# A four-layer kernel on one core: the first half sequence's state-space preparation, issued beside the attention in smaller steps

## The chip, the cores and the metric

One NeuronCore of a Trainium2 chip runs the whole kernel in one launch. The metric is the time of one execution in device microseconds. All arithmetic is fp32. TensorE does the matrix products, VectorE and ScalarE the elementwise work on SBUF and PSUM, GpSimd elementwise work on SBUF and indirect transfers, and SyncE issues most other transfers.

## The reference

Four layers run one after another on x of shape (4, 1024, 128), each an attention-like part and a feed-forward part, with a layer norm behind each part. The change lies where the third layer meets the fourth.

- Layer 2 (the third), first part: a causal linear attention with 16 heads of 64, its queries and keys put through a ReLU and weighted by cos and sin of the position. Second part: a mixture of 8 experts of which each token takes 2.
- Layer 3 (the fourth), first part: a selective state-space model. Each token row is scaled by its root mean square, projected to 256 channels, put through a causal convolution of width 4 and a SiLU; then

```
delta = softplus(wd2 @ (wd1 @ xs) + b)        # 256 channels x time
B, C  = wb @ xs, wc @ xs                       # 16 states x time
h_n(t) = exp(delta(t) * A_n) * h_n(t-1) + delta(t) * xs(t) * B_n(t)
y(t)   = sum_n C_n(t) * h_n(t) + W_D * xs(t)   # gated, projected, added
```

  Second part: 8 experts of width 512 with a top-p choice, computed for every token.

## The kernel before, in words

The sequence of each of the 4 batches is cut in two for layer 3: eight half sequences of 512 tokens. Tokens lie on partitions in `xN[b]`; `xT[b]` is the transposed copy, features on partitions.

**Order of work.** The kernel is a set of Python generators, each of which emits some instructions up to its next `yield`. The loop in `l2_attn` runs over t; one turn is called a unit here. There are 128 units (16 quarters of 256 tokens times 8 pairs of heads), in a pipeline: turn t emits, in this order on TensorE, the transposes of the keys of unit t+1 (`l2_keys`, tile kp_mo), the projection of unit t+2 (`l2_project`, pqk), the scores of t+1 (pa_m, masked by VectorE into `a`), the products with the state and within the block of unit t (po), and the running sums of t+1 (kp_mo, added by VectorE into `st`). Then comes one tile of layer 2's experts for an earlier batch (`early(moe)`), then one call of `begin`, then the division by the normaliser (`l2_out`: dn, co), then the generators in `side`: values of the next quarter (pv), output projection (transposes pt<-co, ScalarE's copy coT, pr), a layer norm, and after a batch's last quarter its dispatch to the experts, which ends in 16 indirect scatters on GpSimd (xrows<-xN). The tile scheduler may reorder what VectorE, ScalarE and GpSimd get, by a plan of the times; in the attention TensorE keeps the written order. Each engine executes its instructions in the order it got them.

`self.beat` is the last ReLU of the newest projection (r_k<-pqk on ScalarE). The scatters already have a dependency on it ("spread out"), so that one goes out with each unit.

**PSUM in the attention.** There are 8 banks: two of tag pj (used by turns for pqk, pv, the transposes pt, the dispatch and the preparation), two for po, one for pr, three for the scores, the keys and sums, and the expert tiles.

**The preparation.** `l3_prepare(u)` makes a half sequence ready for the scan: squares and root mean square (L1754 to L1759), scaling (L1761), transposes and xnT (L1766 to L1769); for each of two groups of 128 channels a projection (pxe), the convolution on VectorE (L1786 to L1802), Tanh (L1806) and xs (L1807); the small projection pdb with db (L1815) and the store of its B and C rows to DRAM (L1816); then for each group delta: the projection pd, softplus as max(p, 0) + log1p(exp(-|p|)) with a correction for rounding (L1826 to L1839), ud = xs * delta (L1840) and the copy of delta to dl (L1841). For seven halves this runs during the scan of the half before. The first half has none before it, so `l2_attn` calls its preparation (`begin`, made by `l3_early`) once a unit as soon as the first batch has left layer 2's experts. `l3_early` places its working tiles in parts of `xT[0]`, `xT[1]`, `xT[2]` that are not read any more. Its PSUM banks are of tag pj, and a bank is worked in until the last step that uses it: the convolution and Tanh stay in pxe, softplus in pd.

**After the attention.** `l3` runs the scans. For every state n GpSimd multiplies ud by a broadcast row of B (L1876: db<-ud,bn; for the first half the tile reads db<-xT,bn), ScalarE takes the exponential (L1880), VectorE scans (L1881), GpSimd multiplies by a row of C (L1892), TensorE sums over n (pys). Layer 2's remaining expert tiles, their gathers on GpSimd (L1556: yg<-yrows) and layer 3's experts (ph, hh, py) are woven in.

Of the kernel before, what the change touches and what calls it, by code (L numbers as in the profile page):

```python
# [42 lines left out]
E3, NST, DDELTA, KCONV = 256, 16, 64, 4  # L43
# [5 lines left out]
SYNC = mybir.DependencyInfo(mybir.DependencyClass.Sync, mybir.DependencyReason.DATA)  # L49
# [22 lines left out]
class Net:  # L72
# [874 lines left out]
    def l2_attn(self, load, dispatch, moe, first):  # L947
# [7 lines left out]
        with ExitStack() as ctx:  # L955
# [35 lines left out]
            for t in range(-2, n + 4):  # L991
                if t == 0:
                    load()
                if 0 <= t + 1 < n:
                    u = units[t + 1]
                    if u["hp"] == 0:
                        i = (t + 1) // NP2
                        if i + 1 < len(quarters):
                            nxt = quarters[i + 1]
                            self.l2_tiles(nxt, quarters[i])  # L1000
                            side.append(self.l2_values(nxt))
                    self.l2_keys(u)
                if 0 <= t + 2 < n:
                    self.l2_project(units[t + 2])
                if 0 <= t + 1 < n:
                    self.l2_scores(units[t + 1])
                if 0 <= t < n:
                    self.l2_before(units[t])
                    self.l2_within(units[t])
                if 0 <= t + 1 < n:  # L1010
                    self.l2_sums(units[t + 1])
                if "put" in self.m2["st"][0] if t > 0 else False:
                    early(moe)
                    if "done" in self.m2["st"][0]:
# [12 lines left out]
                for g in side[:]:  # L1027
                    if next(g, self) is self:
                        side.remove(g)
            for g in (begin, *side):  # L1030
                for f in g:
                    if f == "put":
                        self.m2["rest"] = g
                        break
# [490 lines left out]
    def l2_expert_out(self, u, units, i, wp):  # L1525
# [12 lines left out]
        if j % 4 == n - 1:  # L1538
# [4 lines left out]
                in_=ys[:, 0:n, :],  # L1543
            )

    def l2_combine(self, st, wp):

        nc, b = self.nc, st["b"]
# [172 lines left out]
    def l3_early(self, pool):  # L1721


        half = lambda b, i: self.xT[b][:, i * 512 : (i + 1) * 512]
        k = [0]

        def at(name, shape):
            if name in ("xnT", "tail", "xs3"):
                return pool.tile(shape, F32, name=name)
            if name in ("dl", "ud"):  # L1730
                return self.xT[1 if name == "dl" else 2].rearrange("p (e t) -> p e t", e=2)
            if name == "sq3":
                return half(2, 0).rearrange("p (k d) -> p k d", d=D)
            if name == "db1":
                return half(2, 1)[0:ND]
            if name == "xc":
                k[0] += 1
                return half(0, k[0] % 2)
            return half(0, name == "sp_w")[:, None, :]

        u = dict(b=0, h=0, at=at, ff=self.bank("pj"))
        self.c3["first"] = u
        return u

    def l3_prepare(self, u):
# [2 lines left out]
        at, ff, dp = u.get("at", self.l3_at), u.get("ff", self.bank("ff")), c3["dp"]  # L1748
        wdb = c3["we"][:, :, 0:ND]

        sq = at("sq3", [P, 4, D])
        ms = self.sm.tile([P, 4], F32, name="ms3")
        for k in range(4):
            nc.scalar.activation(  # L1754
                sq[:, k, :], self.xN[b][:, 4 * h + k, :], AF.Square, accum_out=ms[:, k : k + 1]
            )
        yield
        nc.scalar.activation(ms, ms, AF.Sqrt, bias=self.epsc, scale=1.0 / D)
        nc.vector.reciprocal(ms, ms)  # L1759
        for k in range(4):  # L1760
            nc.scalar.activation(  # L1761
                sq[:, k, :], self.xN[b][:, 4 * h + k, :], AF.Copy, scale=ms[:, k : k + 1]
            )
        yield
        pt = ff([P, 4, P], "pt")
        for k in range(4):  # L1766
            self.tr(pt[:, k, :], sq[:, k, :])
# [2 lines left out]
            xnT, pt.rearrange("p a b -> p (a b)"), AF.Copy, scale=self.col("norm_w")  # L1770
        )
        yield

        K1 = KCONV - 1
        tail = at("tail", [P, 2, K1]) if h == 0 else u["prev"]["tail"]
# [2 lines left out]
        for ec in range(2):  # L1778
            p = ff([P, 512], "pxe")
            self.mm(p, c3["wskip"][:, 1, ec * P : (ec + 1) * P], xnT)  # L1780
            xc = at("xc", [P, 512])
            i = 2 * KCONV + ec
            w = [c3["cw"][:, j : j + 1] for j in range(ec * KCONV, (ec + 1) * KCONV)]
            bias = c3["cw"][:, i : i + 1]
            o = K1 if h else 0
            nc.vector.tensor_scalar(xc[:, o:], p[:, o:], w[K1], bias, ALU.mult, ALU.add)  # L1786
            if h:
                nc.vector.scalar_tensor_tensor(
                    xc[:, 0:K1], p[:, 0:K1], w[K1], tail[:, ec, :], ALU.mult, ALU.add
                )  # L1790
            for d in range(1, KCONV):
                nc.vector.scalar_tensor_tensor(
                    xc[:, d:], p[:, 0 : 512 - d], w[K1 - d], xc[:, d:], ALU.mult, ALU.add
                )
            if h == 0:
                nc.vector.tensor_scalar(
                    tail[:, ec, :], p[:, 512 - K1 :], w[0], bias, ALU.mult, ALU.add
                )
                for d in range(K1 - 1, 0, -1):
                    nc.vector.scalar_tensor_tensor(  # L1800
                        tail[:, ec, 0:d], p[:, 512 - d :], w[K1 - d], tail[:, ec, 0:d],
                        ALU.mult, ALU.add,  # L1802
                    )
            yield

            nc.scalar.activation(p, xc, AF.Tanh)  # L1806
            nc.vector.scalar_tensor_tensor(xs[:, ec, :], p, 1.0, xc, ALU.add, ALU.mult)  # L1807
            yield

        db = at("db1", [ND, 512])  # L1810
        rows = dp.tile([2 * NST, 512], F32, name="rows")
        p = ff([ND, 512], "pdb")
# [4 lines left out]
        yield  # L1817

        dl, ud = at("dl", [P, 2, 512]), at("ud", [P, 2, 512])
        for g in ((0,), (1,)) if "at" in u else ((0, 1),):  # L1820
            us, v = at("sp_u", [P, len(g), 512]), at("sp_w", [P, len(g), 512])
            p2 = []
            for k, ec in enumerate(g):
# [11 lines left out]
            for k, ec in enumerate(g):  # L1835
                p = p2[k]
# [2 lines left out]
                nc.vector.tensor_add(p, v[:, k, :], p)  # L1839
                nc.vector.tensor_mul(ud[:, ec, :], xs[:, ec, :], p)  # L1840
                nc.scalar.copy(dl[:, ec, :], p)  # L1841
            if g[-1] == 0:
                yield
        u.update(xnT=xnT, xs=xs, dl=dl, ud=ud, rows=rows)

    def l3_scan(self, u):
# [400 lines left out]
```

## Time and profile before

| what | us |
|---|---|
| median of 9 runs (lowest to highest) | 2262.88 (2253.77 to 2266.32) |
| the profiled execution | 2262.4 |
| its span, first to last instruction | 2260.6 |
| first and last projection of the attention (start) | 594.6, 1295.4 |
| first half's projections: pxe, pdb, last pd (start) | 1247.8, 1269.1, 1289.1 |
| last scatter of the last batch (start) | 1367.4 |
| first product of the scan stage on GpSimd (start) | 1364.9 |
| last product of the scan stage on GpSimd (start) | 2120.4 |
| busy: TensorE, VectorE, ScalarE, GpSimd | 1990.8, 1363.6, 1185.9, 1023.8 |

The page gives one profiled execution: busy times by engine, the span in 40 slices, and groups of instructions. The other views are answers of the same trace: the chain of waits that ended last, the timeline of an engine (start, length, engine, line, what is written and read, and in brackets the idle time before it with what ended that), and busy times in chosen windows. Times are from the start of the span. A tile of the first half that lies in a transposed input is named xT there.

### The profile page before, as it was taken

The page shows a single profiled execution, that of the slowest core. Times are in us where ns is not written, and L with a number is a line of the kernel's source. Part 1 is how long each engine was busy: PE and PEld are TensorE (multiplying, and loading weights), DVE is VectorE, ACT ScalarE, POOL GpSimd, SP SyncE. Part 2 cuts the span into 40 slices and gives each one's busy share as a digit, 9 for nine tenths or more (in the row PEclk, how much of TensorE's full clock was granted, in tenths as well). Part 3 has the DMA queues.
Part 4 walks back from the last instruction along what each step waited for, and adds up shares of the span by engine and source line. Part 5 has one row for each costly group of instructions (what it writes and reads, how often), then busy time and mean ns, then how long its engine had stood idle before and what let it go on. Part 6 is the DMA issues. An engine that isn't in the chain of part 4 may idle for free.

```text
span 2260.6 us, 46328 instructions
## 1 busy us (share of the span) xinstructions
PE 1990.8 (88%) x17791; PEld 1395.1 (62%) x17791; DVE 1363.6 (60%) x3705; ACT 1185.9 (52%) x2578; POOL 1023.8 (45%) x813
## 2 busy tenths in 40 slices
PE   7689889999999999999979876689898999999998
PEld 3576555544577777787758664356565656565666
DVE  7767644433455654755655555686877688686522
ACT  6532443322344444444555556476768787677443
POOL 5100410000123244234143329989798889789400
PEclk9768988989999999999999987799999999999999
DMA  3010110050000010031222056466776676676421
GB/s 107 0 38 10 31 38 1 19 176 0 1 3 3 2 39 22 25 87 40 76 80 87 17 176 211 124 190 194 212 209 171 185 186 189 182 203 176 108 61 52
DMA packets 138604, 211.04 MB, mean 93 GB/s; under 512 B 18644, under 2 KB 75981, under 8 KB 137998
## 3 DMA queue, kind: packets, MB, share of 16 engines
q1 hardware_dynamic: 126238, 173.81, 24.9%
q0 software_dynamic: 12144, 34.26, 7.2%
q8 instruction: 140, 2.29, 0.4%
q14 instruction: 82, 0.67, 0.1%
HBM read 160.22 MB, written 23.16 MB: 81 GB/s over the span
## 4 chain that ended last, share of the span: by engine, by line
PE 44%; DVE 13%; ACT 11%; issue 3%; POOL 1%; DMA 1%; SPq 0%; DVEq 0%; POOLq 0%; ACTq 0%
PE py L140 8%; PE ph L140 7%; PE po L1153 5%; PE pqk L140 5%; PE pa_m L140 5%; DVE db L1881 4%; PE kp_mo L140 3%; PE pv L140 2%; PE pr L1223 2%; PE pys L140 2%; ACT da L1880 1%; ACT hh L2007 1%; PE pt L144 1%; PE kp_mo L144 1%; ACT xN L187 1%
## 5 line engine op out<-in xcount | busy, mean ns | idle before, releaser
L1086 POOL TENSOR_TENSOR qt<-r_q,sb_c_turn 128x256 f32<-128x256 f32 (+1 forms) x256 | 164.3, 662 | 449.2 <-ACT r_q L1078 445.4
L1892 POOL TENSOR_TENSOR hc<-db,cn 128x1024 f32<-128x1024 f32 x128 | 321.3, 2544 | 62.7 <-PE pys L140 28.2
L140 PEld LDWEIGHTS py<-wh,hh 128*128 128x128 f32 x2048 | 255.0, 195 | 79.0 <-issue 47.1
L1876 POOL TENSOR_TENSOR db<-ud,bn 128x1024 f32<-128x1024 f32 x112 | 294.1, 2685 | 7.6 <-ACT dl L1841 5.1
L140 PE MATMUL ph<-xT,wh 128*128 128x512 f32 x512 | 255.5, 617 | 24.5 <-ACT hh L2007 7.1
L140 PE MATMUL py<-wh,hh 128*128 128x128 f32 x2048 | 262.2, 279 | 10.8 <-ACT hh L2007 4.2
L2007 ACT ACTIVATE hh<-ph,sb_cols 128x512 f32<-128x512 f32 x256 | 170.3, 681 | 118.7 <-PE ph L140 92.4
L1144 DVE TENSOR_TENSOR a<-pa_m,sb_c_near 128x256 f32<-128x256 f32 x256 | 96.8, 420 | 201.3 <-PE pa_m L140 201.3
L1101 ACT ACTIVATE kN<-kp_mo,sb_c_trig 128x128 f32<-128x128 f32 x448 | 130.2, 372 | 131.4 <-PE kp_mo L144 123.2
L1880 ACT ACTIVATE da<-dl,aneg 128x512 f32<-128x512 f32 x224 | 153.6, 690 | 74.5 <-DVE db L1881 73.8
L140 PE MATMUL pys<-hc,sb_c_ident 128*128 128x512 f32 x324 | 157.7, 615 | 22.2 <-POOL hc L1892 19.5
L1881 DVE TENSOR_TENSOR_SCAN db<-da,carry,db 128x512 f32<-128x512 f32 x128 | 157.0, 1267 | 21.7 <-POOL db L1876 11.4
L1881 DVE TENSOR_TENSOR_SCAN db<-da,db 128x512 f32<-128x512 f32 x128 | 149.5, 1207 | 11.7 <-ACT da L1880 6.4
L140 PEld LDWEIGHTS ph<-xT,wh 128*128 128x128 f32 x512 | 89.0, 196 | 105.9 <-issue 49.5
L2032 DVE SCALAR_TENSOR_TENSOR h_acc<-py,gt,h_acc 128x128 f32<-128x128 f32 x252 | 70.8, 343 | 123.3 <-PE py L140 123.3
L140 PE MATMUL pqk<-xT,wE 128*128 128x256 f32 x512 | 136.0, 389 | 8.3 <-ACT coT L1220 4.2
L140 PEld LDWEIGHTS pys<-hc,sb_c_ident 128*128 128x128 f32 x324 | 60.0, 198 | 84.0 <-issue 56.1
L140 PEld LDWEIGHTS pqk<-xT,wE 128*128 128x128 f32 x512 | 88.3, 193 | 21.8 <-DVE cv L1063 8.0
L1220 ACT COPY coT<-pt 128x512 f32<-128x512 f32 x64 | 37.6, 587 | 114.8 <-PE pt L144 114.8
L140 PE MATMUL po<-ht,wD 128*128 128x512 f32 x192 | 92.9, 594 | 0.0
L1153 PE MATMUL po<-cv,a 128*64 128x65 f32 x2048 | 89.1, 230 | 0.0
L1556 POOL DMA_INDIRECT yg<-yrows,di x64 | 61.2, 956 | 57.3 <-DVE ch L1388 36.8
(463 smaller groups left out, 4265.1 us busy)
## 6 DMA issues: line engine op xcount, KB each, us to landing
wx<-in_wF SPq DMA_DIRECT2D x92, 384.0 KB, 3.4
bn<-rows SPq DMA_DIRECT2D x128, 256.0 KB, 4.6
cn<-rows SPq DMA_DIRECT2D x128, 256.0 KB, 4.1
wh<-in_wH SPq DMA_DIRECT2D x64, 512.0 KB, 3.6
hc<-hc POOLq DMA_DIRECT2D x47, 512.0 KB, 6.7
xrows<-zero SPq DMA_DIRECT2D x4, 1472.0 KB, 12.1
xg<-xrows SPq DMA_DIRECT2D x20, 256.0 KB, 3.2
yrows<-ys SPq DMA_DIRECT2D x20, 256.0 KB, 3.3
```

The costliest lines, as they stand in the source:

```text
L140: return self.nc.tensor.matmul(out=out, lhsT=lhsT, rhs=rhs, start=start, stop=stop)
L1086: nc.gpsimd.tensor_mul(u["qt"][:, m, a:], u["q"][:, a:], c2["turn"][:, m, o + a : o + 2 * P])
L1101: self.nc.scalar.activation(u["kN"][:, c, m, :], pk[:, c, :], AF.Copy, scale=trig[:, k, m : m + 1])
L1144: nc.vector.tensor_mul(u["a"][:, i, :, :], pa[i], self.c2["near"][:, None, :].to_broadcast([P, 2, P]),)
L1153: self.nc.tensor.matmul(out=u["po"][self.HALF[j], i, c, :], lhsT=lhsT, rhs=rhs, start=key not in u["begun"], stop=True, skip_group_check=True,
L1556: nc.gpsimd.indirect_dma_start(out=yg[h][:, k, c, :], out_offset=None, in_=st["out"][:, :], in_offset=bass.IndirectOffsetOnAxis(ap=st["des ...
L1876: nc.gpsimd.tensor_mul(db, ud, bc[0])
L1880: nc.scalar.activation(da, dl[:, ec, :], AF.Exp, scale=aneg[:, j : j + 1])
L1881: nc.vector.tensor_tensor_scan(db[:, ec, :], da, db[:, ec, :], carry[:, ec, n : n + 1] if h else 0.0, ALU.mult, ALU.add,)
L1892: nc.gpsimd.tensor_mul(hc, db, bc[1])
L2007: nc.scalar.activation(ht, ph, AF.Relu, bias=self.col("h_b1", i=e * NK + k))
L2032: nc.vector.scalar_tensor_tensor(acc[:, c, :], py[:, c, :], gt[:, c, e : e + 1], acc[:, c, :], ALU.mult, ALU.add,)
```

## The change

Four things are edited; all but the first concern only the first half's preparation (`early` is true when `u` comes from `l3_early`).

1. The loop calls `begin` a second time at the end of each unit.
2. The preparation has more `yield`s: 30 calls run it through, where 12 did. A new helper `pace` gives an instruction a dependency on `self.beat`, the newest unit's last ReLU; most of the preparation's instructions on ScalarE and VectorE get it.
3. pxe is copied by ScalarE to a tile in SBUF (`tmp`), and convolution, Tanh and xs work from there. In softplus, pd is read twice (Abs, max) and not used again; the rest works in `sp_u`, `sp_w`, `tmp` and dl, so that dl needs no copy. `sp_u`, `sp_w` and `tmp` lie in the pool of the dispatch (`moed`) instead of `xT[0]`.
4. Softplus takes both channel groups up to exp, then one logarithm over both, then the sums.

```diff
@@ l2_attn, end of the loop over t
                 for g in side[:]:
                     if next(g, self) is self:
                         side.remove(g)
+                if begin is not None:
+                    next(begin, None)
@@ new
+    def pace(self, i):
+
+        self.tc.add_manual_dep(i.ins, self.beat.name, SYNC, reason="spread out")
+        return i
@@ l3_early, at()
             if name in ("xnT", "tail", "xs3"):
                 return pool.tile(shape, F32, name=name)
+            if name in ("sp_u", "sp_w", "tmp"):
+                return self.m2["md"].tile(shape, F32, name=f"e_{name}")
...
-            return half(0, name == "sp_w")[:, None, :]
@@ l3_prepare
+        early = "at" in u
+        pace = self.pace if early else (lambda i: i)
...
-            nc.scalar.activation(
-                sq[:, k, :], self.xN[b][:, 4 * h + k, :], AF.Square, accum_out=ms[:, k : k + 1]
-            )
-        yield
-        nc.scalar.activation(ms, ms, AF.Sqrt, bias=self.epsc, scale=1.0 / D)
-        nc.vector.reciprocal(ms, ms)
+            pace(
+                nc.scalar.activation(
+                    sq[:, k, :], self.xN[b][:, 4 * h + k, :], AF.Square, accum_out=ms[:, k : k + 1]
+                )
+            )
+            if early and k == 1:
+                yield
+        yield
+        pace(nc.scalar.activation(ms, ms, AF.Sqrt, bias=self.epsc, scale=1.0 / D))
+        if early:
+            yield
+        pace(nc.vector.reciprocal(ms, ms))
         for k in range(4):
...
+            if early and k % 2 == 0:
+                yield
+            pace(
+                nc.scalar.activation(
+                    sq[:, k, :], self.xN[b][:, 4 * h + k, :], AF.Copy, scale=ms[:, k : k + 1]
+                )
+            )
+        yield
+        if early:
+            yield
         pt = ff([P, 4, P], "pt")
...
         yield
+        if early:
+            yield
...
             p = ff([P, 512], "pxe")
             self.mm(p, c3["wskip"][:, 1, ec * P : (ec + 1) * P], xnT)
+            if early:
+                t = at("tmp", [P, 512])
+                nc.scalar.copy(t, p)
+                p = t
+                yield
...
-            nc.vector.tensor_scalar(xc[:, o:], p[:, o:], w[K1], bias, ALU.mult, ALU.add)
+            pace(nc.vector.tensor_scalar(xc[:, o:], p[:, o:], w[K1], bias, ALU.mult, ALU.add))
...
             for d in range(1, KCONV):
-                nc.vector.scalar_tensor_tensor(
-                    xc[:, d:], p[:, 0 : 512 - d], w[K1 - d], xc[:, d:], ALU.mult, ALU.add
+                if early and d == 2:
+                    yield
+                pace(
+                    nc.vector.scalar_tensor_tensor(
+                        xc[:, d:], p[:, 0 : 512 - d], w[K1 - d], xc[:, d:], ALU.mult, ALU.add
+                    )
                 )
...
-            nc.scalar.activation(p, xc, AF.Tanh)
-            nc.vector.scalar_tensor_tensor(xs[:, ec, :], p, 1.0, xc, ALU.add, ALU.mult)
-            yield
-
+            pace(nc.scalar.activation(p, xc, AF.Tanh))
+            if early:
+                yield
+            pace(nc.vector.scalar_tensor_tensor(xs[:, ec, :], p, 1.0, xc, ALU.add, ALU.mult))
+            yield
+
+        if early:
+            yield
         db = at("db1", [ND, 512])
...
-        for g in ((0,), (1,)) if "at" in u else ((0, 1),):
+        if early:
+            yield
+            us, v = at("sp_u", [P, 2, 512]), at("sp_w", [P, 2, 512])
+            t = at("tmp", [P, 2, 512])
+            for ec in range(2):
+                p = ff([P, 512], f"pd{ec}")
+                self.mm(p, c3["wd2"][:, ec * P : (ec + 1) * P], db[0 : DDELTA + 1, :])
+                nc.scalar.activation(us[:, ec, :], p, AF.Abs)
+                nc.vector.tensor_single_scalar(dl[:, ec, :], p, 0.0, ALU.max)
+                yield
+                pace(nc.scalar.activation(us[:, ec, :], us[:, ec, :], AF.Exp, scale=-1.0))
+                pace(
+                    nc.scalar.activation(
+                        v[:, ec, :], us[:, ec, :], AF.Identity, bias=self.ones[:, 0:1]
+                    )
+                )
+                yield
+            for ec in range(2):
+                pace(
+                    nc.scalar.activation(t[:, ec, :], v[:, ec, :], AF.Identity, bias=c3["neg1"])
+                )
+            yield
+            pace(nc.scalar.activation(v, v, AF.Ln))
+            for ec in range(2):
+                yield
+                d = dl[:, ec, :]
+                pace(nc.vector.tensor_sub(t[:, ec, :], us[:, ec, :], t[:, ec, :]))
+                pace(nc.vector.tensor_add(d, d, t[:, ec, :]))
+                pace(nc.vector.tensor_add(d, v[:, ec, :], d))
+                pace(nc.vector.tensor_mul(ud[:, ec, :], xs[:, ec, :], d))
+        for g in () if early else ((0, 1),):
...
-            if g[-1] == 0:
-                yield
```

More of the change, by code (lines that the diff above doesn't have):

```diff
@@ L1753, in l3_prepare @@
         for k in range(4):
-            nc.scalar.activation(
-                sq[:, k, :], self.xN[b][:, 4 * h + k, :], AF.Square, accum_out=ms[:, k : k + 1]
+            pace(
[10 more added lines that the diff above has]
+        pace(nc.vector.reciprocal(ms, ms))
+        for k in range(4):
+            if early and k % 2 == 0:
[4 more added lines that the diff above has]
+                )
             )
         yield
-        nc.scalar.activation(ms, ms, AF.Sqrt, bias=self.epsc, scale=1.0 / D)
-        nc.vector.reciprocal(ms, ms)
-        for k in range(4):
-            nc.scalar.activation(
-                sq[:, k, :], self.xN[b][:, 4 * h + k, :], AF.Copy, scale=ms[:, k : k + 1]
-            )
-        yield
+        if early:
+            yield
         pt = ff([P, 4, P], "pt")
```

## The prediction

> **What bounds the kernel now.** I read the page's slices first, to see which stage the change lies in and what follows it.
>
> ```profile
> PE   7689889999999999999979876689898999999998
> POOL 5100410000123244234143329989798889789400
> PEclk9768988989999999999999987799999999999999
> ```
>
> A slice is 56.5 us. The attention fills slices 10 to 22 (600 to 1307 us), with TensorE at nine tenths. Slice 22 (1243 to 1300) drops to 8: there the first half's preparation runs. From slice 24 on GpSimd has the most to do: in the windows of the trace it is busy 672 of the 751 us from 1365 to 2116, and TensorE then works off a rest until 2254. A delay before 1365 should be passed on whole to the end, and so should a gain.
>
> Next the chain of waits over 1240 to 1300 (start, length, what).
>
> ```profile
> 1247.87 1.07 PE pxe L140 x2
> 1248.96 0.82 DVE xT L1786
> 1249.81 0.76 DVE xT L1792
> ...
> 1253.45 0.61 ACT pxe L1806
> 1254.09 0.69 DVE xs L1807
> 1256.09 0.87 PE pqk L140 x4
> ...
> 1278.97 0.69 ACT pd L1832
> 1279.68 1.28 ACT L1833
> ...
> 1281.63 0.70 DVE pd L1839
> 1283.86 2.07 PE pqk L140 x4
> ```
>
> Elsewhere the chain is TensorE alone. Here it leaves TensorE for the convolution, Tanh, softplus and a table load (L1833), and comes back only with the next projection. The timeline of TensorE gives the holes (in brackets the idle time before the row):
>
> ```profile
> 1255.79 0.30 PE L144 MATMUL kp_mo<-sb_c_ident,r_k 128*128 128x128 f32 x1 [2.74 <-DVE st L1128]
> 1282.71 0.48 PE L144 MATMUL pt<-sb_c_ident,co 128*128 128x128 f32 x1 [3.48 <-DVE co L1198]
> 1283.86 2.07 PE L140 MATMUL pqk<-xT,wE 128*128 128x256 f32 x4 [0.46 <-ACT coT L1220]
> 1294.88 1.27 PE L140 MATMUL pqk<-xT,wE 128*128 128x256 f32 x4 [3.18 <-ACT coT L1220]
> ```
>
> VectorE, in order, had st and co queued behind preparation work that itself waited for ScalarE. With two gaps of 0.56 and 0.44 the idle time is 10.9 us. After the two longest gaps the same matmuls are slower (pqk 2.07 against 1.03). In the windows the granted clock is 0.53 over 1283.8 to 1289.2 and 0.63 over 1294.8 to 1299.4. Row by row against warm units this adds 2.5 and 1.7. So the preparation costs the attention 15.0 us in stalls, between 1239.44 and 1302.11.
>
> Last the timeline of GpSimd, for what waits on the attention's end:
>
> ```profile
> 1297.81 1.42 POOL L1086 TENSOR_TENSOR qt<-r_q,sb_c_turn 128x256 f32<-128x256 f32 x2 [9.74 <-ACT r_q L1078]
> 1336.06 0.99 POOL L1556 DMA_INDIRECT yg<-yrows,di  x1 [36.84 <-DVE ch L1388]
> ...
> 1346.20 0.99 POOL L1410 DMA_INDIRECT xrows<-xN,di  x1 [0.30 <-DVE wt L1404]
> ...
> 1364.91 2.36 POOL L1876 TENSOR_TENSOR db<-xT,bn 128x1024 f32<-128x1024 f32 x1
> ```
>
> The scan's first product (1364.91) stands behind eight gathers and 15 of 16 scatters. The scatters wait for the last batch's dispatch, which hangs on the attention's last unit; the gathers wait for expert tiles, one per unit. The scan's inputs are ready far earlier: dl at 1299.4.
>
> **The change, part by part.** The sum is made against the profiled execution, 2262.4 us (span 2260.6, 1.8 around it); the median, 2262.88, is 0.5 higher.
>
> *Where the calls fall.* Before, call 3 of the preparation (transposes) is in the unit whose pqk starts at 1239.44, one call a unit, call 12 in that at 1294.88. Counted through the diff there are now 30 calls, two a unit: transposes at 1244.69, the convolutions' matmuls at 1249.87 and 1266.20, pdb at 1283.86, pd0 at 1294.88, and pd1, the rest of softplus and ud in the three units after the last projection. I number units by these old starts.
>
> *What goes: the stalls.* TensorE's own work in the window is 62.7 - 15.0 = 47.7 us, and 46.7 without pd1 (0.96). The ceiling is thus 16.0 up to 1302, or 15.0 with pd1 paid afterwards. pxe and pd are let go after one copy or two reads (0.6 to 1.3 us) instead of 6 to 10 us, and the longest paced step on VectorE is 2.2 us.
>
> *What the small steps still cost.* Attention's own VectorE work in such a unit is 1.6 us (a 0.66, dn 0.33, co 0.34, st 0.28). Unit 1255.92 gets a whole convolution: 0.8 + 3 x 0.75 + 0.27 + 2 x 0.2 = 3.7, together 5.35 against 3.58 of TensorE: 1.8 late. The unit at 1271.87, with 3.0 of TensorE, cannot go below the shortest full unit of the trace, 3.9: 0.9. Together 2.7, leaving 13.3. The bounds are 0, if it fits between, and 5.4, twice this, if each step also delays the next key transpose.
>
> *Sqrt.* Before, L1758 shared the table load at 1158.87 with a layer norm. Paced, it comes in the unit at 1233.23, where expert tiles with Tanh run: two loads of 1.28. A like pair at 1227.32 and 1228.93 left TensorE idle for 2.17 at 1231.61, so I take 2.2 (0 to 2.6).
>
> *Logarithm.* Before it took loads Ln, Exp, Ln and back to Tanh; now one Ln (128x1024; the row of that size, L1828, is 1.06) and the way back. The number of loads stays four with Sqrt. But Ln now falls between expert tiles of the attention's tail: 1.28 + 1.06 + 1.28 = 3.6 on ScalarE. I take 2 (0 to 3.6), since ScalarE stood idle for 1.6 to 2.0 ahead of each such tile's sg.
>
> *The last eight tensor_tensors*, 8 x 0.69 = 5.5 us on VectorE, come beside the last quarter's norm; I take 1 (0 to 5.5, less likely since they stand in two steps). Their operands move from PSUM to SBUF: L1585 has 691 ns with PSUM and 684 without, so nothing. The two added copies (L1220: 0.59) replace two dl copies (0.59): nothing.
>
> *Waits added.* On ScalarE a paced instruction follows r_k on its own engine: no wait. On VectorE it waits for r_k with a, dn, co and st behind it; a needs matmuls queued after the same pqk, so the wait itself costs nothing, only the step's length, counted above. *Queues moved past:* the store of rows (SP) goes from 1271.78 to some 1282, with an xg load (1282.07) and weight loads (1301.21) behind it and its reader at 1346.12; nothing. GpSimd gets none of the steps. *Memory:* the working tiles move from the transposed input into space of their own; no wait on the old places shows in the rows, so nothing.
>
> *Sum.* 13.3 - 2.2 - 1.0 (pd1) - 2 - 1 = 7.1 us at the last unit. The dispatch, gathers, scatters and first product follow by the same amount, since dl (then about 1308) has some 50 us to spare: 2262.4 - 7.1 = 2255.3, stated as 2255. With every cost at its low end 2262.4 - 15.0 = 2247; with all at the high end 15.0 - 5.4 - 2.6 - 3.6 - 5.5 = -2.1, so 2264.5.
>
> A rule weighed against a row: the gaps of 3.48 and 3.18 us were each followed by a lowered clock, worth 4.2 us together. The Trainium skill ("TensorE: Matmul & The Clock Gate", Part 1) has the clock fall to half after an idle window of about 3.4 us, and advises against gaps longer than that. By that length alone only the first gap should cost clock and the ceiling would be 13.3 instead of 15.0; the measured 0.63 after 3.18 decides for me.
>
> Another that speaks against separate table changes: the ScalarE rows here show 1.28 a load. The Trainium skill ("ScalarE: Activation LUTs", What ACT_TABLE_LOAD costs) adds a drain of 1.38 to each. By that the Sqrt and Ln terms would be about 5 us dearer and the sum about 2261.
>
> **The rivals.**
>
> *Gain lost at the queue* (no change, 2262). GpSimd's first work after the attention, the gathers at 1336, needs the expert tiles, and four waits for their weights cost TensorE 13.0 us between 1302 and 1366. If weights set the tiles' pace, tiles begun 7 us earlier end when they did and the first product stays at 1365. Against it: no weights were asked for between 1238 and 1301, so the stream starts earlier too.
>
> *The steps are exposed* (slower, 2272). The same work, spread, can hold up every unit instead of some. It is about 16 us on VectorE (two convolutions 7.7, xs and max 2.8, softplus 5.5) and 18 on ScalarE with its loads: 34. Place: the units from 1225 to the end, where st and kN wait in order behind steps. With 16.0 recovered and a share s exposed the change is 34s - 16.0: it turns slower at s = 0.47, and at three quarters it is +9.5. Before, 15 of the 34 were exposed; my sum has about a quarter. For it: fp32 units without an expert tile have only 3.3 us of TensorE, so no room.
>
> *Other order in the scan stage* (2265, either side of no change). The instruction order there is planned. If the next eight gathers (1375.57 to 1385.3, 10.0 us) come before the first product, the start is 7.1 earlier and 10.0 later: +2.9. With products ahead of scatters it would gain as much.
>
> *It doesn't do what it says*: if planned steps still cluster, the stalls stay; it falls under "no change".
>
> **How the numbers follow.** This kernel's runs before spread by 0.5%, and about 0.2% (4.5 us) can be told from no change. Forecast 0.62 (below 2258 0.53, same 0.08, slower 0.01, by its costs between 2247 and 2264.5), lost at the queue 0.12 (same), exposed 0.16 (slower), other order 0.10 (0.04, 0.03, 0.03). That makes faster 0.57, same 0.23, slower 0.20. The range reaches from 2245 (costs at nothing, products early) to 2268 (half of the exposed case): 2 in 10 outside. The forecast's own range is 2247 to 2264.
>
> **What would show it.** Right: gaps over 2.5 us gone from TensorE between 1240 and 1300, granted clock near 1.0 there, last po matmul at about 1300 instead of 1306.8, first db product at about 1358, GpSimd's stretch after that as long as before (751). One Ln load instead of two, a Sqrt load at about 1235. Wrong: gaps moved to the units with convolutions, the first product at 1365 in spite of an earlier attention, or a scan stage longer than 751 us.

## The result: 2274.1 us, slower by 0.67%, and the profile after

The changed kernel takes 2274.11 us (median of 19 runs, 2271.49 to 2280.83); the kernel before, in 62 runs, 2259.59. The ratio of the runs is 1.0067, 95% interval [1.0058, 1.0077]; the medians differ by 14.5 us. The forecast was 2255, its range ended at 2268. The profiled executions compared here have spans of 2260.6 (before) and 2275.1 us (after).

The page's slices after, one digit for 56.9 us:

```profile
PE   6778889899899999999979856688898889898998
POOL 5100411000223244234143339989888779889500
PEclk9778979899999999999989978799999999999999
```

Slice 22 (1251 to 1308, the end of the attention) still reads 8 on TensorE, slice 23 behind it has fallen from 7 to 5, and in slices 31 and 32 (1763 to 1877) TensorE has fallen from 9 to 8 and GpSimd from 8 to 7. I read both traces by milestones (starts, us):

| | before | after | difference |
|---|---|---|---|
| U, projection of the 12th unit from the end | 1225.2 | 1223.7 | -1.4 |
| last projection (pqk) | 1294.9 | 1289.1 | -5.7 |
| last po matmul | 1306.7 | 1302.0 | -4.7 |
| first gather (yg) | 1336.1 | 1336.5 | +0.4 |
| first product on GpSimd (db) | 1364.9 | 1365.3 | +0.3 |
| last product on GpSimd (hc) | 2120.4 | 2136.0 | +15.6 |
| end | 2260.6 | 2275.1 | +14.5 |

(The last projection's time is the start of its first matmul; the 1295.4 given of before is the start of a later one.) U is where the calls of the preparation begin. From there the attention gained 4.3 us, the tail up to the first gather lost 6.2 (41.2 to 47.4), and the scan stage, first to last product, grew from 755.5 to 770.7.

The chain of waits over 1240 to 1300 after (start, length, what):

```profile
1255.53 0.47 ACT r_q L1080
1256.00 0.37 ACT r_k L1080
1256.40 0.76 DVE xT L1815
1257.16 0.66 DVE a L1146 x2
1257.82 0.67 DVE xT L1824
1258.52 0.75 DVE xT L1824
1259.34 0.20 DVE st L1127
1259.54 0.66 DVE xT L1824
1260.19 0.10 DVE dn L1199
1260.32 0.43 DVE co L1200
1260.80 0.33 PE pt L144
```

Tanh and the table loads have left the chain, and softplus stands in it only behind the last projection (1294.5 to 1299.2). What remains in the attention is a whole convolution (L1815, three times L1824) in one unit, begun on the signal r_k, with `a`, st, dn and co of the attention between its steps, and the second convolution in a later unit. TensorE's timeline shows what that leaves, and below it the tail:

```profile
1260.80 0.33 PE L144 MATMUL pt<-sb_c_ident,co 128*128 128x128 f32 x1 [2.98 <-DVE co L1200]
...
1277.43 0.30 PE L144 MATMUL kp_mo<-sb_c_ident,r_k 128*128 128x128 f32 x1 [2.64 <-DVE dn L1199]
...
1305.58 0.71 PE L140 MATMUL pa_m<-xgT,wx 128*128 128x128 f32 x4 [1.04 <-DVE mh L1523]
1309.69 1.23 PE L140 MATMUL pa_m<-xgT,wx 128*128 128x128 f32 x4 [3.40 <-DVE mh L1523]
```

The gaps of 2.74, 3.48 and 3.18 us are gone, two of 2.98 and 2.64 stand in the two convolution units, and three new ones behind the last projection: 0.95 at 1299.4, where softplus's sums on VectorE stood ahead of st, and the two shown. ScalarE's timeline for these two:

```profile
1303.70 0.25 ACT L1519 ACTIVATE sg<-pa_m 128x128 f32<-128x128 f32 x1
1303.97 1.28 ACT L1879 ACT_TABLE_LOAD   x1
1305.27 1.06 ACT L1879 ACTIVATE e_sp_w<-e_sp_w 128x1024 f32<-128x1024 f32 x1
1306.34 1.28 ACT L1519 ACT_TABLE_LOAD   x1
1307.64 0.28 ACT L1519 ACTIVATE sg<-pa_m 128x128 f32<-128x128 f32 x1
```

The one logarithm lies between two tiles of layer 2's experts. The second tile's pa_m, itself 1.04 late, ended at 1306.3; its sg starts at 1307.64, behind the table load. VectorE then has two of softplus's sums (0.68 each, L1885 and L1886) between its part of sg (1307.95) and mh (1309.36), and TensorE waits for mh. GpSimd's first work after the attention answers to the gathers and the first product shown of before:

```profile
1336.48 0.99 POOL L1563 DMA_INDIRECT yg<-yrows,di  x1 [44.20 <-DVE ch L1390]
...
1365.25 2.35 POOL L1941 TENSOR_TENSOR db<-xT,bn 128x1024 f32<-128x1024 f32 x1
```

So nothing of the attention's gain reaches the scan stage, and the 14.5 us are lost inside it.

### The profile page after: what moved, and what is told of

Read it like the earlier page. It is cut to its first block, busy times and chain, and to the rows that moved or that the text cites. A ratio compares the mean times of both kernels' runs of the same rounds, so it can differ in the third digit from the quotient of the medians.

```text
span 2275.1 us, 46320 instructions
## 1 busy us (share of the span) xinstructions
PE 1989.5 (87%) x17791; PEld 1392.2 (61%) x17791; DVE 1362.6 (60%) x3705; ACT 1179.6 (52%) x2575; POOL 1025.4 (45%) x813
## 4 chain that ended last, share of the span: by engine, by line
PE 43%; DVE 14%; ACT 9%; issue 3%; POOL 2%; DMA 2%; SPq 0%; DVEq 0%; ACTq 0%; POOLq 0%
PE py L140 7%; PE ph L140 7%; PE po L1155 5%; DVE db L1946 5%; PE pqk L140 5%; PE pa_m L140 4%; PE pys L140 3%; PE kp_mo L140 3%; PE pr L1225 2%; PE pv L140 2%; PE pt L144 1%; ACT hh L2072 1%; ACT da L1945 1%; PE kp_mo L144 1%; ACT L177 1%
## 5 line engine op out<-in xcount | busy, mean ns | idle before, releaser
L1957 POOL TENSOR_TENSOR hc<-db,cn 128x1024 f32<-128x1024 f32 x128 | 314.9, 2484 | 76.6 <-PE pys L140 33.5
L1941 POOL TENSOR_TENSOR db<-ud,bn 128x1024 f32<-128x1024 f32 x112 | 287.6, 2611 | 8.6 <-ACT dl L1908 5.1
L140 PE MATMUL pys<-hc,sb_c_ident 128*128 128x512 f32 x324 | 162.9, 633 | 22.5 <-POOL hc L1957 19.9
L2097 DVE SCALAR_TENSOR_TENSOR h_acc<-py,gt,h_acc 128x128 f32<-128x128 f32 x252 | 71.1, 343 | 125.2 <-PE py L140 125.0
## 6 DMA issues: line engine op xcount, KB each, us to landing
xrows<-zero SPq DMA_DIRECT2D x4, 1472.0 KB, 12.2
```

The lines of the kernel that those rows point to most:

```text
L140: return self.nc.tensor.matmul(out=out, lhsT=lhsT, rhs=rhs, start=start, stop=stop)
L1941: nc.gpsimd.tensor_mul(db, ud, bc[0])
L1957: nc.gpsimd.tensor_mul(hc, db, bc[1])
L2097: nc.vector.scalar_tensor_tensor(acc[:, c, :], py[:, c, :], gt[:, c, e : e + 1], acc[:, c, :], ALU.mult, ALU.add,)
```

## Where the scan stage loses them

I compared the starts of its 128 products (db) in the two profiled executions, each counted from the first one. At every fourth product, after minus before is -7.1 to +2.8 us up to product 72 (-0.1 there), +9.0 at product 76, +16.4 at 80, and 15.8 to 21.8 from then on. The step lies at 1800 to 1870 us. What GpSimd waited for over 1780 to 1870, in total, times and longest, first before, then after:

```profile
POOL hc L1892 <- PE pys L140: 5.7, 2, 4.1
POOL hc L1892 <- DVE db L1881: 2.0, 1, 2.0
```

```profile
POOL hc L1957 <- PE pys L140: 16.4, 4, 7.2
POOL hc L1957 <- ACT da L1945: 4.6, 1, 4.6
```

A product hc needs a buffer that a sum over the states (pys on TensorE) lets go. TensorE's timeline after, at the step:

```profile
1802.35 5.67 PE L140 MATMUL py<-wh,hh 128*128 128x128 f32 x26 [3.62 <-ACT hh L2072]
1807.86 1.88 PE L140 MATMUL ph<-xT,wh 128*128 128x512 f32 x4
1809.58 1.88 PE L140 MATMUL pys<-hc,sb_c_ident 128*128 128x512 f32 x4
...
1817.98 4.72 PE L140 MATMUL py<-wh,hh 128*128 128x128 f32 x26 [3.28 <-ACT hh L2072]
1822.54 1.88 PE L140 MATMUL ph<-xT,wh 128*128 128x512 f32 x4
1824.26 1.88 PE L140 MATMUL pys<-hc,sb_c_ident 128*128 128x512 f32 x4
```

The pys sums stand behind 26 py and 4 ph matmuls of an expert, and those wait for hh. Before, the sums of the first block stood ahead of its 26 py, and the 26 py of the two blocks waited 0 and 0.55 us for hh:

```profile
1795.85 1.88 PE L140 MATMUL pys<-hc,sb_c_ident 128*128 128x512 f32 x4
1797.71 3.17 PE L140 MATMUL py<-wh,hh 128*128 128x128 f32 x26
...
1806.39 3.17 PE L140 MATMUL py<-wh,hh 128*128 128x128 f32 x26 [0.55 <-ACT hh L2007]
```

ScalarE's timeline after shows what hh is queued behind:

```profile
1795.08 0.67 ACT L2072 ACTIVATE hh<-ph,sb_cols 128x512 f32<-128x512 f32 x1
1795.77 1.28 ACT L177 ACT_TABLE_LOAD   x1
...
1797.23 0.68 ACT L2072 ACTIVATE hh<-ph,sb_cols 128x512 f32<-128x512 f32 x1
1797.80 1.64 ACT L187 ACTIVATE xN<-ss_r,ln_nm,ln_rs 128x128 f32<-128x128 f32 x4
...
1799.71 1.28 ACT L1945 ACT_TABLE_LOAD   x1
...
1801.63 0.67 ACT L2072 ACTIVATE hh<-ph,sb_cols 128x512 f32<-128x512 f32 x1
```

A layer norm with its two table loads lies among the hh. That alone is not new: before, the same norm and its loads (1788.49 and 1790.07) lie among hh too, and TensorE had sums to do meanwhile. The code that emits the scan stage is the same in both kernels, instruction for instruction. What differs is the order the planner gave each engine. Counted in the traces from the stage's first pys as number 0, pys number 188 is TensorE's matmul number 1504 before and 1530 after; pys number 196 is number 1616 and 1646: 26 and 30 more matmuls ahead of the same sums. For the groups of four pys that follow each, the difference is 0 and -2, so the count doesn't explain the second block's wait of 3.28.

## The experiments

Theory A: the planned order of the scan stage costs the time. Theory B: the preparation's own steps and the disturbed expert tiles cost it. To tell them apart I wrote an order out as a list of the stage's instructions for each engine, and tied neighbours by a dependency of order only, which adds no wait:

```diff
+        at = len(tc.nc.cur_bb.bb.instructions)
         n.l3(moe, fp)
+        in_order(tc, list(tc.nc.cur_bb.bb.instructions)[at:])
@@ in_order, for the listed rows of an engine
+        for a, b in zip(row, row[1:]):
+            tc.add_manual_dep(
+                b,
+                a.name,
+                mybir.DependencyInfo(mybir.DependencyClass.NoSync, mybir.DependencyReason.DATA),
+                reason="in order",
+            )
```

These runs were on other chips than the first ones, on which the kernel before takes 2293 to 2298 us (the control's scan stage there: 775.7), so each is read by its ratio to the kernel before on its own chip.

**The control: before with its own order written out.**

> The kernel before, with its own order of the scan stage written out as a list instead of left to the planner: the same instructions in the same order on every engine. Every theory: ratio 1.000 to the kernel before. It gives the trace of before on the chip of these experiments: last projection, first gather, first product and the length of GpSimd's scan stage there (estimates from the run with the new order on this chip, whose attention is unchanged: 1308, 1348, 1377; length 775 to 780).

Measured: 0.9992 [0.9979, 1.0006]. U to last projection 71.1 us, on to the first gather 41.1, stage 775.7.

**The change as it is, on such a chip.**

> The changed kernel as it is, on the chip of these experiments. Theory A (the planned order of the scan stage is what costs): the loss of before is found again, ratio 1.004 to 1.007, and the trace's scan stage is 8 to 15 us longer than the 776 of the kernel before on this chip, the difference arising between products 64 and 84. Theory C (the loss belongs to the one chip on which it was first measured): 0.999 to 1.001.

Measured: 1.0045 [1.0029, 1.0062]; stage 788.7, 13.0 longer than the control's. Against the control its products stand at -0.4 us at product 72, +9.2 at 76, +15.0 at 80: the step of the first chip at the same products. Theory C falls. U to last projection is 65.4 (5.7 shorter than the control), on to the first gather 46.8 (5.7 longer): the sum, 112.2, is that of the control, 112.1.

**The change with the order of before, and before with the order of the change.**

> The changed kernel whole, but in the scan stage (all that is emitted after the attention) every engine gets its instructions in the order in which the kernel before has them; edges between neighbours on an engine impose it, without a wait. Theory A, the planned order of the scan stage costs the time: the first product on GpSimd stays near 1365 (the last unit's gain is lost in the tail), the stretch from the first to the last product falls from 770 to about 755, and the time is that of the kernel before within 0.25% (2255 to 2265 where before is 2260). Theory B, the preparation itself or the place of its tiles slows the scan stage, whatever the order: 2270 to 2278.

Measured: 1.0003 [0.9991, 1.0016], stage 779.8. The step is gone: +3.9 at product 72, +3.9 at 80. With the order of before the change neither gains nor loses.

> The kernel before, but in the scan stage every engine gets its instructions in the order in which the changed kernel has them. Theory A, the order: slower than before by 0.4 to 0.8% (2269 to 2278 where before is 2260), with the delay again between products 72 and 84 of the scan stage. Theory B, the preparation: no difference from before (2256 to 2264).

Measured: 1.0042 [1.0026, 1.0059], stage 785.8, the attention as in the control; -0.1 at product 72, +6.4 at 76, +12.2 at 80. So the order alone makes the kernel before as slow as the change. Theory B falls.

**One engine's order at a time** (the list of in_order cut to that engine).

> The changed kernel, with only GpSimd's order in the scan stage as before; the other four engines are planned anew around it. Theory A1 (GpSimd's order of products is what costs): ratio to before 0.999 to 1.002, like the run in which all engines had the old order (1.0003). Theory A2 (the order of the others, expert tiles and scans on TensorE, VectorE and ScalarE, is what costs): 1.004 to 1.007.

> The changed kernel, with the old order of the scan stage on TensorE, VectorE, ScalarE and SyncE; only GpSimd is planned anew. Theory A1 (GpSimd's order of products is what costs): 1.003 to 1.007. Theory A2 (the order of the others is what costs): 0.999 to 1.002.

Measured: 1.0003 [0.9988, 1.0017] with GpSimd's old order, 0.9998 [0.9982, 1.0015] with that of the four others. Either list takes the loss away; the planner moves the rest too, and the pair doesn't separate the theories. The second has a stage of 776.2, as the control. The first has 786.8, in a profiled execution that is among its slowest (2308.1, median 2299.8), so its trace can't be set against its median. In that trace TensorE has 26 and 22 matmuls more than before ahead of the two sums counted above, and the stage loses 7.5 us between products 72 and 84 (5.3 to 12.8). Why its median shows no loss all the same stays open, so the misplaced matmuls by themselves don't settle the size of the loss.

> The changed kernel with the old order of the scan stage on TensorE alone; the four other engines are planned anew around it. In the changed kernel's trace GpSimd's products wait for pys sums that stand on TensorE behind 26 py and 4 ph matmuls, which themselves wait 3.3 to 3.6 us for hh. Theory A2 (that order of TensorE's queue is what costs): ratio to before 0.999 to 1.002 and no such waits. If the order of another engine is enough to lose the time: 1.003 to 1.007.

Measured: 0.9995 [0.9976, 1.0013], stage 772.6, with everything in the attention and its tail as in the change (65.4 and 46.8). The step is gone (-3.2 at product 72, -1.4 at 80). The windows over 1820 to 1850 (length, then busy time of TensorE, its weight loads, VectorE, ScalarE, GpSimd, then the granted clock, DMA share and GB/s), first of the change on these chips, then with TensorE's old order:

```profile
1820.00:1850.00 30.00, 23.08 (x97) 16.85 (x96) 19.37 (x43) 20.89 (x39) 23.96 (x13) 0.84 0.57 150
```

```profile
1820.00:1850.00 30.00, 27.85 (x129) 17.04 (x128) 24.29 (x48) 26.66 (x50) 26.56 (x14) 1.00 0.70 204
```

In these 30 us every engine gets more done, and the clock stays at 1.00. The waits for hh ahead of the 26 py are now 0.89 and 0.55 us:

```profile
1829.30 3.17 PE L140 MATMUL py<-wh,hh 128*128 128x128 f32 x26 [0.89 <-ACT hh L2072]
...
1837.98 3.17 PE L140 MATMUL py<-wh,hh 128*128 128x128 f32 x26 [0.55 <-ACT hh L2072]
```

and the 26 matmuls take 3.17 us instead of 5.92 and 4.79 (the change on these chips).

> The changed kernel with TensorE's old order for 264 matrix products only, those between the 93rd and the 112th pys product (scan products 72 to 84 or so); ahead of them its plan is that of the changed kernel, and all else is planned. Theory A3 (30 more py and ph matmuls ahead of the pys sums in that stretch cost the time): the step of 15 us between products 72 and 84 goes, the stage is within 4 us of that of the kernel before on this chip (772 to 780), ratio 0.999 to 1.002. If the loss comes from the order over the whole stage, it comes back elsewhere: 1.003 to 1.007.

Measured: 1.0016 [1.0002, 1.0029], stage 784.1. From product 72 to 84 it loses 3.0 us (5.1 to 8.1) where the change loses 16.0 (-0.4 to 15.6). Losses elsewhere, 4.5 between 64 and 68 and 3.7 behind product 120, stand in the change's trace too (4.5 and 2.9). The profiled execution is the slowest of its twelve (2309.8, median 2302.5), so its stage can't be set against the ratio. By the ratios (1.0045 to 1.0016, on two chips) the stretch holds about two thirds of the loss; their intervals allow anything from a fifth to all of it.

> The kernel before, with TensorE's order in the scan stage that of the changed kernel, the other four engines planned around it. Theory A2 (TensorE's order is enough): the step appears between products 72 and 84, stage 784 to 792, ratio 1.003 to 1.007. If it takes other engines' orders too: 0.999 to 1.002.

Measured: 1.0110 [1.0087, 1.0133], stage 798.8; GpSimd's waits in this kernel over 1780 to 1920:

```profile
POOL hc L1892 <- PE pys L140: 28.8, 6, 10.4
```

TensorE's order alone is more than enough, with an attention like the control's (71.0 and 40.7). Of the 23.0 us of stage, 13.2 come between products 72 and 80 (8.6 to 21.7). Others come ahead of the stretch (+12.7 at product 64, 8.6 at 72); that the other engines, planned around a foreign order, fit it worse there is my guess.

**The parts of the change, all with the order of before.** The banks alone, with the working tiles where the change has them:

```diff
@@ l3_prepare of the kernel before
             self.mm(p, c3["wskip"][:, 1, ec * P : (ec + 1) * P], xnT)
+            if "at" in u:
+                t = at("tmp", [P, 512])
+                nc.scalar.copy(t, p)
+                p = t
...
                 nc.vector.tensor_single_scalar(dl[:, ec, :], p2[k], 0.0, ALU.max)
+                if "at" in u:
+                    p2[k] = at("tmp", [P, 512])
```

> The kernel before with one part of the change alone: the projection pxe is copied by ScalarE to a tile in SBUF at once, softplus works in tiles in SBUF after two reads of pd, and the working tiles lie where the change puts them; twelve calls, one a unit, one logarithm for each channel group, no pacing. The order of the scan stage is that of before, so that only the attention and its tail can move. My sum put the banks' share of the stalls at little, since VectorE's queue ends the two long waits: by it the gaps of 2.7, 3.5 and 3.2 us stay and the ratio is 0.998 to 1.001. If the stalls come from the banks, the last two gaps go and the last projection is 6 to 10 us earlier against its start than before: 0.996 to 0.998.

Measured: 1.0003 [0.9987, 1.0018]. Gaps of 2.88 and 3.45 us on VectorE's st and co remain; the third, of 3.18 ahead of the last projection, is not there, but one of 2.32 on st stands behind it. U to last projection is 68.0 (3.1 shorter), on to the gather 44.5 (3.4 longer). So the banks cost little, and VectorE's queue ends the waits that remain.

No pacing (`pace` returns its instruction as it is), and three calls a unit instead of two:

```diff
                 if begin is not None:
-                    next(begin, None)
+                    for k in range(2):
+                        next(begin, None)
```

> The changed kernel with the old order in the scan stage, and without the added dependency on the newest unit's last ReLU; the small steps, the tiles in free memory and the early return of banks stay. If VectorE's waits for that ReLU hold up the attention's own work (it stood idle 0.7 and 1.7 us for r_k ahead of convolution steps, with st and co behind), the last projection starts 2 to 4 us earlier than with it (1289 to about 1286 us). If the length of the steps alone does it, the start stays within 1 us, or gets later because the planner bunches the steps again. Time: within 5 us of the run with the dependency.

> The changed kernel with the old order in the scan stage, and three calls of the preparation a unit instead of two, so that softplus is over before the expert tiles come back in the attention's last units. If the logarithm and the eight sums among those tiles eat the gain (TensorE stood idle 1.0 and 3.4 us for mh at 1305 and 1309), the gather on GpSimd that came at 1336 comes 3 to 6 us earlier relative to the last projection, and the time falls 3 to 6 us below the run with two calls. If the tail is bound by expert weights, nothing moves. Against it: more steps a unit, which can cost 2 to 4 us before the last projection.

Measured: no pacing 0.9970 [0.9955, 0.9984]; U to last projection 63.5, on to the gather 47.7, together 0.9 less than the control. The gap in the first convolution's unit is 2.60 instead of 2.98, so the length of the steps makes most of it and the wait for r_k little. Its stage is 5.4 us shorter than the control's, 3.0 of it by a step between products 60 and 64, which I can't explain. Three calls 0.9984 [0.9969, 0.9998]: 71.2 and 38.0, stage 780.6. With the last softplus steps back in the attention the tail is 9.3 us shorter than with two calls and the same order (47.3), and the attention 7.7 longer: most of it only changes its place.

> The changed kernel without the pacing (pace returns the instruction as it is), with the scan stage planned freely. With the order of before it ran at 0.997. The plan here is nearer to that of before than the changed kernel's plan is. Theory A (the order decides): 0.997 to 1.000. If small edits of the preparation cost by themselves and the order only comes on top: 1.002 to 1.007, as with the change.

Measured: 1.0016 [1.0000, 1.0033]. The window from U to the gather is the one of no pacing with the order of before (111.1 and 111.2), the stage is 780.7 against 770.4. My expectation was too low: an order that looked close to that of before still went with some 10 us more of stage, half of which is the shortening that no pacing had against the control. TensorE's counts ahead of the two sums are those of before here, and there is no step between products 72 and 80 (+8.9 and +9.0 against no pacing): the time is lost in another place.

> The changed kernel with both edits that gained: three calls of the preparation a unit instead of two (the last softplus steps leave the attention's tail), no pacing, and the order of the scan stage as before. If the two gains (0.997 and 0.9984) have different places and add up: 0.994 to 0.997, first product 6 to 12 us nearer to the last projection than the 69.8 of the kernel before with its own order on this chip, last projection no later against its start than with two calls (695 to 699 us). If three steps a unit are too many for VectorE: 0.998 to 1.000, with the gaps on TensorE grown to over 12 us in sum before the last projection.

Measured: 0.9972 [0.9958, 0.9987], the best version here that beats both kernels with its cause in view: U to last projection 67.9, on to the gather 37.2, together 6.9 us less than the control; stage 775.0, as the control; the ratio says 6.4 us. The two gains don't add up, though, and two of my numbers missed: the last projection is 702 us behind the first (695 to 699 expected), the first product 66.1 behind the last projection (57.8 to 63.8 expected). One gap has grown:

```profile
1299.69 0.47 PE L144 MATMUL pt<-sb_c_ident,co 128*128 128x128 f32 x1 [4.11 <-DVE co L1201]
```

> Three calls a unit, no pacing and the old order of the scan stage, as in the run before (0.9972), with each step of the two convolutions in a call of its own. If the stalls left are whole convolutions in one unit on VectorE: the gap of 4.1 us ahead of the last projection goes below 2, the idle time up to the last units falls from 9.1 to about 5, ratio 0.994 to 0.997. If they come from the sum of VectorE's work, however cut: 0.997 to 0.999 and gaps of 2 to 3 us in other units.

Measured: 0.9997 [0.9983, 1.0011]. The gap of 4.11 became 2.60, but others came (2.89 on st, 0.79, 0.78), 10.7 us in sum against 9.1; U to the gather 109.0. My first case fails: cut finer, VectorE's work held up more units.

Seven of these kernels have the old order on every engine in the scan stage, and their stages, one profiled execution each, are 770.4 to 781.3 us long. So a few us between two such stages are no sign of the order. The step of the change, 15 to 17 us within eight products and on two chips, is well above that.

## Why the prediction was wrong, point by point

**The step that failed most is that gathers, scatters and "first product follow by the same amount", with GpSimd's stretch left at its length.** The prediction read the stretch as a fixed length hung on its first product (as 751 us, the length of a window; from first to last product it is 755.5). It isn't fixed: all that follows the attention was planned anew with the edit ahead of it, and with the new plan the stretch took 15.2 us more. The mechanism was among the rivals ("other order in the scan stage"), but in the wrong place and at the wrong price: eight gathers ahead of the first product, +2.9. Gathers and first product kept their order (1336.48, 1365.25); TensorE's queue in the middle of the stage was what moved. The rival had a chance of 0.10, 0.03 of it for slower.

**The small steps: 2.7 us set, 8.7 measured.** The sum took the first convolution's unit as 5.35 of VectorE against 3.58 of TensorE, 1.8 late. The wait was 2.98: the steps begin after r_k (1256.40), `a` comes after the first step, and co stands last (2.60 without the wait for r_k). The second unit, where the second convolution meets the quarter's cr and layer-norm statistics on VectorE, waited 2.64 instead of 0.9 (whose source, a shortest full unit of 3.9, was read too long: the trace has units of 3.74). With 0.25 more that is 5.87 idle, and the clock costs 2.8: pqk, pa_m and po took 1.33, 1.06 and 1.69 us behind the first gap, and pa_m and po 1.06 and 1.93 behind the second, against 0.87, 0.60 and 1.08 in a warm unit. "Granted clock near 1.0" was wrong.

**Sqrt: 2.2 set, about 0.7 measured.** The two loads came where they were expected (1235.46 and 1237.88); that unit is 7.6 us long against 6.2. Of the 1.4, 0.43 is idle time behind the second load and some 0.3 slower matmuls next to it; the other 0.7 is a slower pqk (1.72 against 1.03), begun ahead of both loads. It belongs to a lowered clock that no term foresaw: behind a gap of 2.16 us at 1230 the granted clock was 0.64 over 1230.2 to 1235.0, where before, behind the same gap (2.17), it was 1.00 over 1231.6 to 1236.4. That cost 1.7 us in all, and not through the change: the control has it too (0.66 over 1243.8 to 1248.8).

**The tail: 4.0 set** (1 for pd1, 2 for the logarithm, 1 for the tensor_tensors), **6.2 measured**. The one Ln load came as foreseen. What was missed is that ScalarE and VectorE add up here: the sg behind the logarithm is followed by sums of softplus ahead of mh, and behind TensorE's 3.40 us of idle time the clock is lower (0.79 over 1306 to 1314). The bounds given (0 to 3.6 and 0 to 5.5) held it.

Together the sum said -7.1 at the first gather. Between U and the gather the profile has +1.9, of which 1.7 is the clock just named, and on the other chips 0.1. So even without the new order there was nothing to pass on, as the run with the order of before shows (1.0003).

**Right:** the ends of the three longest waits went (Tanh, softplus, table loads); the calls fell into the units counted; GpSimd's first work waits for the expert tiles; no effect of the banks, of the store of rows or of the copies was seen. "The steps are exposed" is true in part: 8.7 of its 34 us show in the attention. "Gain lost at the queue" named the right result, an unchanged first product, with another cause: not the weights, but softplus among the tiles (without it there, with three calls, the tail is 9.3 us shorter).

**The skill's rules.** The prediction set the row (clock 0.63 behind a gap of 3.18) above the idle window of about 3.4 us in the Trainium skill ("TensorE: Matmul & The Clock Gate", Part 1). The runs have shorter gaps with a lowered clock, and gaps of the same length without it, as the last section shows. The drain of 1.38 that the Trainium skill ("ScalarE: Activation LUTs", What ACT_TABLE_LOAD costs) adds to a load isn't seen: sg ends at 1303.95, the load starts at 1303.97, and Ln starts 1.30 after that. The skill's sum (2261) was nearer to the time, by a cost that the trace doesn't have.

## What to carry to other kernels

Where a planner orders the engines' queues, an edit ahead of a long stage can change that stage's order although its code stays the same. Hold the order fixed in a control run before crediting or blaming the edit, and look at which queue holds the sums that let buffers go: here the order of TensorE's queue alone, which put 26 and 30 matmuls ahead of two groups of them, was enough for more than the whole loss (1.0110). Work taken out of one queue's busy place has to land where the queues that it uses have room together; moved from the attention into its tail it cost the same again.

## What the runs showed of the hardware

A gap well below the 3.18 us of the prediction's row can be followed by a lowered TensorE clock, but its length alone doesn't decide. The windows of the change, before any gap and for 5 us behind the gaps of 2.98 and 2.64 us (the granted clock is the third number from the end):

```profile
1245.00:1250.00 5.00, 5.00 (x102) 4.48 (x101) 2.01 (x7) 2.37 (x8) 2.39 (x3) 1.00 0.06 16
1260.80:1265.80 5.00, 5.00 (x81) 4.11 (x81) 1.97 (x6) 2.58 (x6) 2.36 (x3) 0.66 0.00 0
1277.40:1282.40 5.00, 4.97 (x80) 4.23 (x80) 2.79 (x8) 1.79 (x5) 2.85 (x3) 0.66 0.00 0
```

And of the kernel before, behind its gap of 2.74 us:

```profile
1255.80:1260.80 5.00, 4.67 (x84) 3.38 (x84) 2.46 (x7) 1.88 (x5) 2.40 (x3) 1.00 0.01 3
```

A gap of 2.16 or 2.17 us was followed by 0.64 in the change, by 1.00 in the kernel before and by 0.66 in the control. What decides between them stays open.

And one program differs by chip: with the same order on every engine, the control's scan stage takes 775.7 us where that of before took 755.5 on the first chip. 12.8 of the 20 us arise within the first 12 products. What makes that difference stays open.
